# Scaling a group's samples in one step, and moving sines, residuals, sums and the last expert pick in a Trainium2 kernel

## The chip, the cores and the metric

The kernel runs on one core of one Trainium2 chip. The metric is device time in microseconds (us) of one execution. The core has a matrix engine (TensorE, PE in the profile), a vector engine (VectorE, DVE), a scalar engine for functions and copies (ScalarE, ACT), a general engine (GpSimd, POOL) and DMA queues. Each engine runs its own instructions in program order and waits on the others by semaphores. Matmuls write to PSUM, of which the kernel makes four tiles of two banks each; VectorE and ScalarE read them from there.

## The reference, cut to what matters

64 signals of 80000 samples are cut into 157 frames of 512 (L = 157, D = 512), and each frame goes through a cosine transform (DCT). One layer follows: layer normalisation, an attention by phases with a gate, and a layer of 16 experts of which each signal takes the best one.

```python
h = tokenizer(x)                              # frames @ dct.T            (64, 157, 512)
x = layernorm(h)
key_phase, query_phase = tanh(x @ Wk + bk) * pi, tanh(x @ Wq + bq) * pi
V = x @ Wv + bv
for s in range(4):                            # 4 sets of 8 planes, phasors exp(i phase)
    memory = cumsum(key_ph[s] * V, axis=1)
    total += softmax(set_weights)[s] * real(sum(memory * conj(qry_ph[s])))
retrieved_pos = ...                           # the same with phases of the position
gate = sigmoid(x @ Wg + bg)
total = gate * total + (1 - gate) * sigmoid(pos_weight) * retrieved_pos
h = h + x + (total / norm) @ Wo + bo
y = layernorm(h)
scores = softmax(mean(y, axis=1) @ Wg_ffn + bg_ffn)
idx = argmax(scores)
h = h + scores[idx] * (y @ We[idx] + be[idx])
```

## The kernel before

The signals go in 16 groups of 4 (g = 0 to 15). The tokens of a group lie in five tiles of 128 rows (n = 0 to 3 and TAIL): four signals by 32 tokens each. The DCT is folded into the weights: in group 0 the weights wv, wkq and wg are carried once into the space of the samples (`through_dct`), less their column mean, so that later products take the folded samples `xT` directly, each column times its token's `rstd`. One group's experts run beside the next groups' work, in a fixed order of instructions.

Weights lose their mean in one of two ways: by a matmul behind the transform, or by subtracting it from the raw weights:

```python
def less_mean(total, k, to):
    nc.tensor.matmul(to, tables[:, 6 + k], total, start=False, stop=True)

def centre(raw, total):
    ps = bank()
    nc.tensor.matmul(ps, mean, total, start=True, stop=True)
    sub(raw, raw, ps.unsqueeze(1).to_broadcast([P, C, D]))
```

A tile's way from the samples (the sines are copied by ScalarE, the sums are VectorE's, rstd is GpSimd's, the residual is ScalarE's), and the scaling of its samples:

```python
def embed_statistics(g, n):
    ...
    nc.scalar.copy(sines, odd[:, 1, : P + 1])
    add(by_r[:, 1, :], odd[:, 0, :P], sines[:, :P])
    sub(by_r[:, 3, :], odd[:, 0, 1 : P + 1], sines[:, 1 : P + 1])
    rstd, shift = statistics(h)          # bn_stats, bn_aggr, then rstd and shift on GpSimd
    ...
def embed_res(g, n):
    ...
    nc.scalar.activation(r, h, AF.Identity, bias=shift, scale=rstd1)

def spread(g, n, room=None):             # rstd of a tile's tokens along the free axis, on all partitions
    s["by", n] = tr = bank()[:, :P] if room is None else room
    nc.tensor.transpose(tr, s["rstd", n].to_broadcast([P, P]), ident)

def scale(g, n):
    x, tr = tile_of(s["xT"], n), s.pop(("by", n))
    nc.vector.tensor_tensor(x, x, tr.unsqueeze(1).to_broadcast([P, C, P]), ALU.mult)
```

Group 0 up to its gate (`keep` writes a tile's value and then scales that tile's samples):

```python
def first_values():
    ...
    def keep(n):
        keep_value(0, n)
        spread(0, n)
        scale(0, n)
    ...
    embed(0, 0)
    embed(0, 1)
    ps = bank()[:, : C * 2 * F].rearrange("p (c n) -> p c n", c=C)
    for k in range(C):
        through_dct(raw_kq, k, ps[:, k], stop=False)
        less_mean(total_kq, k, ps[:, k])
    embed_statistics(0, 0)
    nc.scalar.copy(wkq, ps)
    embed_statistics(0, 1)
    ...                                  # residuals, value(0, n), keep(n), embeds of the other tiles
    keep(2)
    next(consts)
    value(0, TAIL)
    fold_once(1, 0)
    centre(raw_g, total)
    keep(3)
    keep(TAIL)
    for k in range(C):
        if k % 2 == 0:
            ps = psum()
        through_dct(raw_g, k, ps[:, k % 2])
        if k % 2:
            nc.scalar.copy(wg[:, k - 1 : k + 1], ps)
    project(0)                           # keys and queries, tanh on ScalarE
    ...
    for n in range(2):
        embed(1, n)
        embed_statistics(1, n)
    phasors(0)                           # eight sines on ScalarE: four for keys, four for queries
    for n in range(2):
        embed_res(1, n)
    weigh()

def first_gate():
    made = chain(weight_sums(wo, t_o), weight_sums(wv, t_v))
    for n in range(C):
        gate_part(0, n)                  # 16 matmuls, tanh on ScalarE
        if n == 0:
            fold_twice(1, 1)
        m = n + 2
        if m < NM:
            embed(1, m)
            embed_statistics(1, m)
        if n == 1:
            scores(0)
        spread(1, n)
        scale(1, n)
        if m < NM:
            embed_res(1, m)
        add_bo(0, n)
        next(made)
        next(made)
    ...
```

The end: the last group's output sums, and the last pick, whose fetched experts end the kernel:

```python
def output_product(g, i):
    ...
    more = lambda to, x: nc.gpsimd.tensor_tensor(to, to, x, ALU.add)
    ...
    elif i == 7:
        add(second, ps, first)
        more(r22, second)
        more(r21, second)
        more(r12, first)

def expert(g, n, between=lambda c: None, spreads=()):
    ps = psum()
    for c in range(C):
        between(c)
        expert_chunk(g, n, c, ps[:, 0, :])
    ...
    expert_out(g, n, ps[:, 0, :])        # result on VectorE, then output DMAs

add_bias(g - 1, ORDER[0])                # g is the last group here
expert(g - 1, ORDER[0])
...
def routes(c):
    ...
    elif c == 3:
        route(g)
        route_sum(g)
...
def picks(c):
    if c == 1:
        route_spread(g)
        pick(g)
        fetch(g, [*flat, all_v.rearrange("p i c o -> p (i c o)")], 2, biases)

add_bias(g - 1, ORDER[1])
expert(g - 1, ORDER[1], routes)
add_bias(g - 1, ORDER[2])
expert(g - 1, ORDER[2], picks)
```

Of the kernel before, what the change touches and what calls it, by code (L numbers as in the profile page):

```python
# [51 lines left out]
def audio_tower(ctx: ExitStack, tc: tile.TileContext, a, out):  # L52
# [158 lines left out]
    def centre(raw, total):  # L211
        ps = bank()
        nc.tensor.matmul(ps, mean, total, start=True, stop=True)
        sub(raw, raw, ps.unsqueeze(1).to_broadcast([P, C, D]))
# [313 lines left out]
    def phasors(g):  # L528
        u = S[g].pop("u")
        for n, to in ((0, kf), (1, qf)):  # L530
            for k in range(2):
                rows = slice(2 * F * k + F * n, 2 * F * k + F * (n + 1))
                to_k = to.rearrange("p s b t -> p (s b t)")[:, HN * k : HN * (k + 1)]
                nc.scalar.activation(to_k[F : 2 * F], u[rows, 0], AF.Sin, scale=PI)
                nc.scalar.activation(to_k[:F], u[rows, 1], AF.Sin, bias=quarter[rows], scale=-PI)
# [75 lines left out]
    def output_product(g, i):  # L611

        s = S[g]
        ps = product(g, i, fac_o)
        (r11, r12), (r21, r22) = ([r[:, :, n : n + H] for n in (0, H)] for r in s["res2"])
        more = lambda to, x: nc.gpsimd.tensor_tensor(to, to, x, ALU.add)  # L616
        if i == 1:
            s["u"] = [p2.tile([P, 2, H], F32, tag="u", name="u") for _ in range(2)]
            nc.scalar.copy(s["u"][0], ps)
        first, second = s["u"]  # L620
        if i in (1, 2):
            add(r11, ps, r11)
        elif i == 6:
            add(first, ps, first)
        elif i == 7:
# [3 lines that stand above are left out]
            more(r12, first)  # L629
        elif i == 5:  # L630
            add(r22, ps, r22)
            if g + 1 == NG:
                add(r12, ps, r12)
            for n in (2, 3):
                statistics2(g, n)
            if g + 1 < NG:
                add(r12, ps, r12)
        elif i == 3:
            add(r12, ps, r12)
        else:  # L640
            add(r21, ps, r21)
# [154 lines left out]
    def expert(g, n, between=lambda c: None, spreads=()):  # L796

        ps = psum()
        for c in range(C):
            between(c)  # L800
            expert_chunk(g, n, c, ps[:, 0, :])
        for k, m in enumerate(spreads):
# [6 lines left out]

    def first_values():  # L810

        consts = constants()

        def keep(n):
            keep_value(0, n)
            spread(0, n)
            scale(0, n)

# [8 lines left out]
        total_kq = add_up(raw_kq, 2 * F, "sum2")  # L827
# [8 lines left out]
        ps = bank()[:, : C * 2 * F].rearrange("p (c n) -> p c n", c=C)  # L836
        for k in range(C):
            through_dct(raw_kq, k, ps[:, k], stop=False)
            less_mean(total_kq, k, ps[:, k])
        embed_statistics(0, 0)  # L840
        nc.scalar.copy(wkq, ps)
# [3 lines left out]
        value(0, 0)  # L845
        fold_once(0, 1, nc.vector)
        fold_twice(0, 1)
        value(0, 1)
        embed(0, 2)
        embed(0, 3)  # L850
        keep(0)
# [5 lines left out]
        keep(1)  # L857
        total = add_up(raw_g, D, "x2T", nc.gpsimd)
        embed(0, TAIL)
        embed_statistics(0, TAIL)  # L860
        embed_res(0, TAIL)
        value(0, 3)
        keep(2)
        next(consts)
        value(0, TAIL)
        fold_once(1, 0)
        centre(raw_g, total)
        keep(3)
        keep(TAIL)
        for k in range(C):  # L870
            if k % 2 == 0:
                ps = psum()
            through_dct(raw_g, k, ps[:, k % 2])
            if k % 2:
                nc.scalar.copy(wg[:, k - 1 : k + 1], ps)
        project(0)
        fold_twice(1, 0)
        fold_phases(0)
        next(consts)
        next(consts)  # L880
        next(consts)
        fold_once(1, 1)
        for n in range(2):
            embed(1, n)
            embed_statistics(1, n)
        phasors(0)
        for n in range(2):
            embed_res(1, n)
        weigh()

    def first_gate():

        made = chain(weight_sums(wo, t_o), weight_sums(wv, t_v))
        for n in range(C):
            gate_part(0, n)
            if n == 0:
                fold_twice(1, 1)
            m = n + 2
            if m < NM:
                embed(1, m)  # L900
                embed_statistics(1, m)
            if n == 1:
                scores(0)
            spread(1, n)
            scale(1, n)
            if m < NM:
                embed_res(1, m)
            add_bo(0, n)
            next(made)
            next(made)  # L910
        spread(1, TAIL)
        scale(1, TAIL)
        add_bo(0, TAIL)
        load_half(2, 0)
# [142 lines left out]
    add_bias(g - 1, ORDER[0])  # L1057
# [6 lines left out]

    def routes(c):
        if c == 1:
            turn_x2(g, 0)
        elif c == 2:
            turn_x2(g, 1, nc.vector.tensor_copy)
        elif c == 3:  # L1070
            route(g)
            route_sum(g)
# [10 lines left out]
    def picks(c):  # L1083
        if c == 1:
            route_spread(g)
# [6 lines left out]
    expert(g - 1, ORDER[2], picks)  # L1092
# [121 lines left out]
```

## Time and profile before

| | |
|---|---|
| time, median of 3 runs | 1423.63 us (1423.09 to 1425.6) |
| span of the profiled run | 1421.9 us |
| TensorE busy | 1405.3 us, 99% |
| VectorE busy | 997.3 us, 70% |
| GpSimd busy | 607.1 us, 43% |
| ScalarE busy | 402.0 us, 28% |
| DMA | 119.74 MB, mean 84 GB/s |

The span runs from the first to the last instruction. A line such as L288 is a line of the kernel file; matmuls are named by their output and inputs (`mm<-ident,rstd`). An entry of a timeline gives start, length, engine, line, operation, and in brackets how long the engine idled before and what released it. Group 0 fills roughly the first 110 us, a steady round of projection, values, gate, experts and attention the time to 1370, and the last group's experts the rest.

### The profile page before, as it was taken

Reading aid. Unit: us, or ns where it says so; the run is one execution under the profiler, and the core shown is the slowest. Engines: PE = TensorE matmul, PEld = TensorE weight load, DVE = VectorE, ACT = ScalarE, POOL = GpSimd, SP = SyncE. Lnnn points to the kernel's source line nnn. Section 1 sums busy time; section 2 is a strip of 40 time slices with the busy share of each in tenths; the row PEclk is TensorE's granted clock in tenths of the full one; section 3 lists DMA queues with packets and bytes.
Section 4 is the critical chain, followed back from the end, with each engine's and each line's share of the span. In section 5 each row is a group of like instructions: output and inputs, shape, how many; then the busy total and the mean of one; then the engine's idle time right before and its main releaser. Section 6 shows DMA issues by size and latency. Waiting matters only on the chain.

```text
span 1421.9 us, 26962 instructions
## 1 busy us (share of the span) xinstructions
PE 1405.3 (99%) x10646; PEld 929.2 (65%) x10646; DVE 997.3 (70%) x2090; ACT 402.0 (28%) x690; POOL 607.1 (43%) x849
## 2 busy tenths in 40 slices
PE   9899999999999999999999999999999999999998
PEld 5477576675757667575675757657586675766762
DVE  5677776777767676677777767677676777767573
ACT  2414242141422314232142422314223142421410
POOL 2354533535444255533535445255442545345322
PEclk9999999999999999999999999999999999999999
DMA  6013204032140322204132040322303232030305
GB/s 219 1 39 125 75 1 177 24 126 75 39 148 16 130 71 109 88 5 167 34 126 75 10 176 16 127 75 76 118 9 134 68 126 74 1 143 22 126 8 192
DMA packets 47485, 119.74 MB, mean 84 GB/s; under 512 B 9264, under 2 KB 26176, under 8 KB 39424
## 3 DMA queue, kind: packets, MB, share of 16 engines
q0 software_dynamic: 11072, 71.31, 13.0%
q1 hardware_dynamic: 35788, 46.06, 11.0%
q8 instruction: 85, 1.39, 0.4%
q10 hardware_dynamic: 500, 0.64, 0.2%
q14 instruction: 40, 0.33, 0.1%
HBM read 97.41 MB, written 20.58 MB: 83 GB/s over the span
## 4 chain that ended last, share of the span: by engine, by line
PE 91%; DVE 3%; POOL 3%; DMA 1%; issue 1%; ACT 0%; SPq 0%; DVEq 0%; POOLq 0%
PE mm L362 26%; PE mm L567 16%; PE mm L778 16%; PE mm L601 9%; PE mm L233 8%; PE mm L674 3%; PE mm L514 2%; PE mm L248 2%; PE mm L250 2%; PE mm L684 1%; POOL rstd L225 1%; PE mm L586 1%; PE mm L548 1%; PE mm L288 1%; DVE st L220 1%
## 5 line engine op out<-in xcount | busy, mean ns | idle before, releaser
L224 POOL TENSOR_SCALAR rstd<-mv 128x1 f32<-128x1 f32 x160 | 53.5, 334 | 536.1 <-DVE mv L222 529.7
L778 PE MATMUL mm<-we,x2T 128*32 128x512 f32 x2400 | 273.2, 595 | 0.5 <-DVE res_t L789 0.5
L778 PEld LDWEIGHTS mm<-we,x2T 128*32 128x32 f32 x2400 | 70.4, 109 | 149.1 <-issue 141.9
L97 DVE TENSOR_TENSOR gT<-mm,gT 128x128 f32<-128x128 f32 (+1 forms) x135 | 87.0, 672 | 88.5 <-PE mm L567 87.0
L609 DVE TENSOR_TENSOR gT<-mm,gT 128x320 f32<-128x320 f32 x256 | 116.9, 487 | 19.1 <-PE mm L601 14.7
L601 PE MATMUL mm<-att,v 32*128 32x192 f32 (+2 forms) x2048 | 127.8, 371 | 0.9 <-ACT res_t L277 0.5
L601 PEld LDWEIGHTS mm<-att,v 32*128 32x128 f32 x2048 | 105.5, 185 | 11.7 <-PE mm L601 2.9
L732 POOL DMA_INDIRECT we<-in_we,rows x60 | 64.3, 1072 | 105.1 <-issue 98.1
L97 DVE TENSOR_TENSOR v<-mm,v 128x512 f32<-128x512 f32 x105 | 70.9, 687 | 52.5 <-PE mm L362 52.5
L577 ACT ACTIVATE gT<-gT,hbg 128x320 f32<-128x320 f32 x120 | 59.6, 554 | 169.0 <-DVE gT L97 169.0
L225 POOL TENSOR_TENSOR rstd<-rstd,power 128x1 f32<-128x1 f32 x160 | 98.6, 616 | 13.4
L97 DVE TENSOR_TENSOR res<-mm,res 128x512 f32<-128x512 f32 x96 | 64.3, 684 | 56.5 <-POOL res L616 41.8
L277 ACT ACTIVATE res<-mm,shift,rstd 128x512 f32<-128x512 f32 x64 | 49.8, 778 | 158.7 <-POOL rstd L263 110.6
L661 ACT ACTIVATE x<-res,shift,rstd 128x512 f32<-128x512 f32 x64 | 52.1, 814 | 139.0 <-DVE res L97 121.9
L362 PE MATMUL mm<-t_o,sum 128*128 128x256 f32 x384 | 88.1, 379 | 0.0
L362 PE MATMUL mm<-t_v,sum 128*128 128x256 f32 x360 | 86.7, 384 | 0.0
L282 POOL TENSOR_TENSOR res<-res,bo 128x512 f32<-128x512 f32 x64 | 86.3, 1377 | 0.2 <-issue 0.2
L789 DVE SCALAR_TENSOR_TENSOR res<-mm,gate,res 128x512 f32<-128x512 f32 x64 | 48.0, 750 | 50.4 <-PE mm L288 36.4
L362 PEld LDWEIGHTS mm<-t_o,sum 128*128 128x128 f32 x384 | 71.9, 190 | 11.0
L616 POOL TENSOR_TENSOR res<-res,u 128x512 f32<-128x512 f32 x48 | 59.6, 1270 | 44.9 <-DVE u L97 44.9
L233 PE MATMUL mm<-wv,xT 128*128 128x512 f32 x160 | 72.0, 594 | 1.1 <-DVE xT L294 0.8
L119 POOL TENSOR_TENSOR xT<-xT 128x640 f32<-128x640 f32 x30 | 46.5, 1550 | 59.7 <-DVE even L97 40.7
(194 smaller groups left out, 2787.8 us busy)
## 6 DMA issues: line engine op xcount, KB each, us to landing
xT<-in_frames SPq DMA_DIRECT2D x32, 640.0 KB, 4.5
out<-res SPq DMA_DIRECT2D x248, 64.0 KB, 1.7
out<-res_t SPq DMA_DIRECT2D x62, 32.0 KB, 1.6
out<-res_t SPq DMA_DIRECT2D x62, 26.0 KB
wv<-in_wv SPq DMA_DIRECT2D x2, 512.0 KB, 5.7
wg<-in_wg SPq DMA_DIRECT2D x1, 1024.0 KB
wo<-in_wo SPq DMA_DIRECT2D x1, 1024.0 KB
we<-in_we,rows POOLq DMA_INDIRECT x60, 8.1
```

The costliest lines, as they stand in the source:

```text
L97: add = lambda *x: nc.vector.tensor_tensor(*x, ALU.add)
L225: nc.gpsimd.tensor_tensor(rstd, rstd, power, ALU.pow)
L233: nc.tensor.matmul(ps, tile_of(x[:, c], n), w[:, c, :], start=(c == 0), stop=(c == C - 1))
L282: nc.gpsimd.tensor_tensor(r, r, bo, ALU.add)
L362: nc.tensor.matmul(ps[:, b, :], lhs[:, c, P * b : P * (b + 1)], w[:, c, :], start=(c == 0), stop=(c == 1))
L567: nc.tensor.matmul(ps[:, o, :HN], w[:, c, o * P : (o + 1) * P], rhs[:, c], start=(c == 0), stop=(c == 1))
L577: nc.scalar.activation(to, to, AF.Tanh, bias=hbg[:, c : c + 1], scale=0.5)
L601: nc.tensor.matmul(to, s["v", n][q, c * P : (c + 1) * P], by, start=(n == 0), stop=(n == TAIL))
L609: nc.vector.tensor_tensor(th, r[:, :, n], th, op)
L616: more = lambda to, x: nc.gpsimd.tensor_tensor(to, to, x, ALU.add)
L732: nc.gpsimd.indirect_dma_start(out=ws[b][:, n * k : n * (k + 1)], out_offset=None, in_=of, in_offset=bass.IndirectOffsetOnAxis(ap=rows[:, ...
L778: nc.tensor.matmul(ps[Q * i : Q * (i + 1), :], s["x2T"][:, c, i, Q * n : Q * (n + 1)], s["ws"][i][:, c, :], start=(c == 0), stop=(c == C - 1),
```

## The change

The first group's samples are no longer scaled tile by tile. All its values are made first from unscaled samples, and `scale_all` then spreads the rstd of all five tiles by six products with the identity and scales two halves at once. The column mean of wkq is taken from the raw weights like that of wg, and both are taken earlier (`means`, `centre`). Around the first gate, the key sines come ahead of the query sines with an embedding between them, residuals move, and the sums of wv's quarters come before those of wo. In the last group, three sums go from GpSimd to VectorE and one expert bias is added earlier. The last pick follows the last chunk of an expert, ahead of that expert's result. The purpose is to keep TensorE from waiting at both ends of the kernel.

```diff
-    def centre(raw, total):
-        ps = bank()
+    def means(total, ps):
         nc.tensor.matmul(ps, mean, total, start=True, stop=True)
-        sub(raw, raw, ps.unsqueeze(1).to_broadcast([P, C, D]))
+    def centre(raw, ps, n):
+        sub(raw, raw, ps.unsqueeze(1).to_broadcast([P, C, n]))
@@ output_product
-        more = lambda to, x: nc.gpsimd.tensor_tensor(to, to, x, ALU.add)
+        last = g + 1 == NG
+        more = lambda to, x: (nc.vector if last else nc.gpsimd).tensor_tensor(to, to, x, ALU.add)
         if i in (1, 2):
             add(r11, ps, r11)
+            if last and i == 2:
+                add_bias(g - 1, ORDER[0])
@@ expert
             expert_chunk(g, n, c, ps[:, 0, :])
+        between(C)
@@ new
+    def scale_all(g):
+        s = S[g]
+        ps = psum()
+        for m in range(2):
+            lo = 0
+            for n, w, at in ((0, P, 0), (1, P, 0), (TAIL, HT, 0)) if m == 0 else ((TAIL, HT, HT), (2, P, 0), (3, P, 0)):
+                nc.tensor.matmul(ps[:, m, lo : lo + w], s["rstd", n].to_broadcast([P, P]),
+                                 ident[:, at : at + w], start=True, stop=True)
+                lo += w
+        for m in range(2):
+            x = half(s["xT"], m)
+            nc.vector.tensor_tensor(x, x, ps[:, m, :HN].unsqueeze(1).to_broadcast([P, C, HN]), ALU.mult)
@@ first_values, from the embeds of tiles 0 and 1 on (the new order; cut)
+        embed_statistics(0, 0)
+        embed_statistics(0, 1)
+        embed_res(0, 0)
+        embed_res(0, 1)
+        value(0, 0)
+        ps = psum()
+        mean_kq, new_kq = ps[:, 0, : 2 * F], ps[:, 1, : C * 2 * F].rearrange("p (c n) -> p c n", c=C)
+        means(add_up(raw_kq, 2 * F, "sum2"), mean_kq)
+        centre(raw_kq, mean_kq, 2 * F)
+        fold_once(0, 1, nc.vector)
+        fold_twice(0, 1)
+        total = add_up(raw_g, D, "x2T", nc.gpsimd)
+        value(0, 1)
+        for k in range(C):
+            through_dct(raw_kq, k, new_kq[:, k])
+        nc.scalar.copy(wkq, new_kq)
+        ...                              # keep_value(0, n) in place of keep(n); embeds, values 2
+        mean_g = bank()
+        means(total, mean_g)
+        centre(raw_g, mean_g, D)
+        value(0, 3)
+        value(0, TAIL)
+        keep_value(0, 3)
+        next(consts)
+        keep_value(0, TAIL)
+        scale_all(0)
+        made = [psum(), psum()]
+        for k in range(C):
+            through_dct(raw_g, k, made[k // 2][:, k % 2])
+        nc.scalar.copy(wg[:, :2], made[0])
+        fold_once(1, 0)
+        fold_twice(1, 0)
+        fold_once(1, 1)
+        project(0)
+        nc.scalar.copy(wg[:, 2:], made[1])
+        fold_phases(0)
+        phasors(0, (0,))
+        next(consts)
+        next(consts)
+        embed(1, 0)
+        embed_statistics(1, 0)
+        phasors(0, (1,))
+        embed_res(1, 0)
+        next(consts)
@@ first_gate
+        made = chain(weight_sums(wv, t_v), weight_sums(wo, t_o))
+        gate_part(0, 0)
+        embed(1, 1)
+        embed_statistics(1, 1)
+        embed_res(1, 1)
+        weigh()
+        fold_twice(1, 1)
+        deviations(0)                    # spread(1, 0), scale(1, 0)
+        add_bo(0, 0)
+        weights()                        # two steps of the weight sums
+        gate_part(0, 1)
+        scores(0)
+        embed(1, 2)
+        embed_statistics(1, 2)
+        deviations(1)
+        embed_res(1, 2)
+        add_bo(0, 1)
+        weights()
+        gate_part(0, 2)
+        for n in (3, TAIL):
+            embed(1, n)
+            embed_statistics(1, n)
+        for n in (3, TAIL):
+            embed_res(1, n)
+        deviations(2)
+        add_bo(0, 2)
+        weights()
+        gate_part(0, 3)
+        add_bo(0, 3)
+        deviations(3)
+        deviations(TAIL)
+        add_bo(0, TAIL)
+        weights()
@@ the end
-    add_bias(g - 1, ORDER[0])
     expert(g - 1, ORDER[0])
     def routes(c):
         ...
         elif c == 3:
             route(g)
             route_sum(g)
-    def picks(c):
-        if c == 1:
+        elif c == C:
             route_spread(g)
             pick(g)
             fetch(g, [*flat, all_v.rearrange("p i c o -> p (i c o)")], 2, biases)
     expert(g - 1, ORDER[1], routes)
     add_bias(g - 1, ORDER[2])
-    expert(g - 1, ORDER[2], picks)
+    expert(g - 1, ORDER[2])
```

## The prediction, as it stood before the run

> **What bounds the kernel now.** I read the page's first part, then the waits of TensorE, then the timelines of the first 96 us and of the last 40. The page:
>
> ```profile
> PE 1405.3 (99%) x10646; PEld 929.2 (65%) x10646; DVE 997.3 (70%) x2090; ACT 402.0 (28%) x690; POOL 607.1 (43%) x849
> ```
>
> TensorE (PE) is busy for 1405.3 of 1421.9 us. From 130 to 1330 us it idles 1.3 us, and the change does not touch that stretch. All that can be won lies in the first 90 us and the last 50. TensorE's waits in the first 96 us ("waited for: total, times, longest"):
>
> ```profile
> PE mm L248 <- issue: 2.6, 1, 2.6
> PE mm L288 <- DVE wg L96: 2.4, 1, 2.4
> PE mm L185 <- POOL ident masks.py:199: 1.4, 1, 1.4
> ...
> PE mm L233 <- DVE xT L294: 0.8, 1, 0.8
> PE mm L601 <- ACT res_t L277: 0.5, 1, 0.5
> ```
>
> L288 is the spreading of a tile's rstd over the partitions: tile 3's stood 2.36 us (43.2 to 45.6) because VectorE (DVE) was centring the gate's weights (L96, 2.29 us), and its bank came free behind that. The largest gap, 61.2 to 63.85, stands before group 1's third tile, behind the sines and residuals on ScalarE (ACT). It costs more than itself, as busy times and granted clock (column after POOL) in stretches of 2 us show:
>
> ```profile
> 62.00:64.00 2.00, 0.15 (x1) 0.18 (x2) 1.20 (x3) 1.53 (x3) 1.81 (x3) 1.00 0.00 0
> 64.00:66.00 2.00, 1.90 (x9) 1.46 (x10) 1.16 (x3) 1.25 (x2) 0.69 (x2) 0.81 0.00 0
> 66.00:68.00 2.00, 2.00 (x6) 1.39 (x5) 0.20 (x1) 1.76 (x3) 0.00 (x0) 0.50 0.00 0
> ```
>
> The gate part that follows takes 5.57 us in the chain instead of 4.31. Before the first read of the values (84.34) I add up, from the waits and the chain: 0.15 + 0.78 + 0.27 + 2.36 + 0.28 + 2.63 + 0.52 waiting, 0.26 (L250 at 16.38, 0.71 instead of 0.45), about 0.5 (L250 at 64.75, on the folding) and 1.26 of slow clock: 9.0 us.
>
> At the end the chain runs through the pick, the fetch and the last expert's matmuls:
>
> ```profile
> 1392.44 7.80 DMA t_v<-in_we,rows
> 1400.24 0.04 issue
> 1400.28 17.37 PE mm L778 x154
> ```
>
> TensorE has finished group 6 at 1395.6 and stands 0.27, 0.90 and 0.44 us for three of the four fetched experts. From 1400.28 it is dense, so the end lies 17.4 + 4.2 us behind the landing of the fourth. VectorE's timeline ahead of the fetch:
>
> ```profile
> 1384.08 0.32 DVE L691 TENSOR_REDUCE tot<-mm 128x1 f32<-128x157 f32 x1 [1.48 <-PE mm L684]
> 1384.94 0.75 DVE L789 SCALAR_TENSOR_TENSOR res<-mm,gate,res 128x512 f32<-128x512 f32 x1 [0.54 <-PE mm L778]
> 1385.61 0.74 DVE L772 SCALAR_TENSOR_TENSOR res<-be,gate,res 128x512 f32<-128x512 f32 x1
> 1386.27 0.22 DVE L708 SCALAR_TENSOR_TENSOR logit<-mm,rbg 128x64 f32<-128x64 f32 x1
> ```
>
> The sums are there at 1384.4, but the pick (L708 on) stands behind an expert's result and the next bias.
>
> **What the Trainium skill says.** "TensorE: Matmul & The Clock Gate", Part 1, has the array fall to half its clock after an idle window of about 3.4 us; here a gap of 2.63 us with sparse work behind it gave 0.50 already, so new gaps of 2 us or more are suspect. "ScalarE: Activation LUTs", What ACT_TABLE_LOAD costs, gives about 1.28 us a load; every load in the trace takes 1.28. Its section on table sets puts cheap functions into every set, and the trace shows no load before a copy or Identity, so sines split by a copy need one load as before. "DMA: Bandwidth & Descriptors", Issuing engines are not separate DMA queues, has all queues share 16 engines; the trace shows them 0.92 to 1.04 busy from 1392 to 1400, so outputs moved into that time delay the fetch.
>
> **The change part by part.**
>
> **Work.** Five spreadings (L288, 0.12 us each in the chain) leave the first values; six identity products, four of 128 columns and two of 64, each two passes of 0.11 or 0.06, come in: 4 x 0.22 + 2 x 0.12 = 1.1, so +0.5 us of TensorE. The eight less-mean matmuls of wkq (0.11 each) leave for two: -0.7. That nets to -0.2. VectorE exchanges five scalings of 0.68 for two of 1280 elements; 1024 take 1.23 and 2048 take 2.29, so some 1.5 each: 3.0 for 3.4. Hardly any work goes; the change must live from waits.
>
> **First values.** I replayed the new order with the trace's durations. The wkq block (17.98 to 20.16 before) moves behind the first values, so value 0 starts near 17.75; VectorE's second statistics start at 18.8 instead of 20.77, because ScalarE's sines no longer stand behind the wkq copy. TensorE then runs value 1 to 25.0, wkq to 26.3, embeds to 28.1, value 2 to 31.6, TAIL's embed to 32.5, the gate's means to 33.3, value 3 to 36.8. VectorE centres wg from 35.8 to 38.1, now beside values instead of before a spreading. Value TAIL may wait 0.7 us for TAIL's residual (ACT, 37.4) and ends at 40.9; the six products end at 42.0, wg's transform (5.43) at 47.4 against 51.6 before, the projection (2.2) at 49.6. The second wg copy, now behind tanh, ends at 51.2. Share (1.0) and one embed (0.9) fill the time, and the first gate part starts at 51.5. Before, it started at 56.74 with one more embed (0.9) behind it: **4.3 us ahead** here.
>
> **First gate.** Here I expect no gain. ScalarE runs the key sines from 52.5, the sines' copy of tile 0, the query sines to 56.9, tile 0's residual (behind POOL's rstd) to 58.8, a table load to 60.1 and tanh to 60.9. TensorE, through its first part at 55.85 and an embed at 56.75, needs tile 0's bank for the next part and stands until 58.8: about 2 us. Tile 1's sines wait for tanh, so VectorE idles until 61.2 and then has no break: statistics, weigh, folding, scaling, two weight sums, two for the scores, and so on, with small waits of TensorE at 66, 73 and 79 (0.6 to 1.3 each, on banks freed by residuals). I get the first read at 80.65 instead of 84.34 (-3.7) and VectorE's first product with the gate (L609) at 82.9 instead of 87.47 (-4.6). L609 sets the reads' pace, 16 x 0.485, so the second counts more: **-4.2 us**.
>
> **Last group's sums.** POOL's three sums take 3.72 us (1368.71 to 1372.43), and VectorE waits 2.61 for the second. On VectorE they take 3 x 0.69 = 2.1, and the next sum starts at 1370.7 instead of 1371.23: -0.5. The bias (L772, 0.72) moves into idle time. So TensorE's 0.45 us wait on res_t (1378.2) goes: **-0.5**.
>
> **Last pick.** The spread of the sums follows chunk 3 directly (0.9 earlier) and the pick follows it on VectorE instead of 0.75 + 0.74 of other work. It starts near 1384.8 instead of 1386.27: with the 0.5 above, 1.5 earlier, and POOL's first fetch too. Against that, this expert's result comes out some 3.3 us behind the pick, at 1388.8, and its 256 KB leave inside the fetch's time instead of before it. At the 270 to 290 GB/s shown there this is up to 0.9 us. I take half: **-1.0 us** at the end, the 0.5 included (TensorE still waits for the data).
>
> Sum: 1423.6 - 4.2 - 1.0 = **1418.4 us**.
>
> **Rivals.** (1) **The gate's new order gives the front's gain back**: TensorE's new stop near 57 lets the clock fall (1.3 us lost, as before), or the chain ScalarE-VectorE-POOL is longer than replayed. For it: ScalarE's table load before tanh stands between two statistics, and small POOL operations have taken double beside VectorE's folding (L224 0.69 at 22.44, else 0.21). Against it: after that stop TensorE has slack, since VectorE is behind. It leaves 1 to 2 us of the front: about 1421. (2) **The fetch is bound by bytes**: starting it earlier then wins nothing. For it: the busy share near 1. Against it: from 1388 to 1390 it was 0.10, room that an earlier start uses. It makes 1419.4. (3) **All gaps close**: the 9.0 us go and the end gives 1.5, so 1413. Against it: the bank that TensorE needs at 57 hangs on a residual which I cannot place before 58. (4) **A bank held too long**: experts' results now leave later, and a fifth tile could stop TensorE; but only one of four is held, so I give it little.
>
> **Range and chances.** The front may give 2 to 6, the end 0 to 1.8. Long replays err towards too much gain, so the range reaches further up: 1415.3 to 1421.5. The three runs before spread over 2.5 us. Faster by over 2% would need 28 us, more than the 16.6 us that TensorE idles in all: 0.01. Slower by over 2% would need a new standstill of 28 us: 0.01. Within 2%: 0.98.
>
> **What would show it.** TensorE's busy time stays within 1 us of 1405; its waits on "DVE wg" (2.4) and on issue before L248 (2.6) are gone; wg's transform ends near 47.4; a wait of 1.5 to 2 us on a residual stands before the second gate part; the first read comes at 80 to 81. At the end, the pick starts near 1380.6 (1386.27 - 4.2 - 1.5), before the expert's result, with no POOL sums in the last group; from the pick to the fourth expert's landing it is now 14.0 us, and I expect 14.5. A gap over 2.6 us with the clock at 0.5 in the gate, or a first read later than 82.5, would prove the front wrong; a landing 15.5 us or more behind the pick would prove the end wrong.

## The result and the profile after

| | before | after |
|---|---|---|
| time, median of 4 runs each | 1424.33 us (1423.09 to 1425.6) | 1418.99 us (1418.3 to 1421.01) |
| ratio after / before, 95% interval | | 0.9965 (0.9948 to 0.9982) |
| span of the profiled run | 1421.9 us | 1419.2 us |

The change makes the kernel 0.35% faster, about 5 us. The profiled run of after is the longest of its four; why will turn out below. First the engines on its page:

```profile
PE 1404.2 (99%) x10647; PEld 929.9 (66%) x10647; DVE 1002.4 (71%) x2091; ACT 401.5 (28%) x690; POOL 602.9 (42%) x846
```

TensorE's busy time fell by 1.1 us only; VectorE's rose by 5.1 and GpSimd's fell by 4.2. Hardly any work went, and the rest of the 2.7 us between the spans are waits. TensorE's waits of after in the first 96 us (total, times, longest):

```profile
PE mm L250 <- ACT res L279: 1.5, 1, 1.5
PE mm L185 <- POOL ident masks.py:199: 1.4, 1, 1.4
PE mm L605 <- ACT res_t L279: 1.1, 1, 1.1
PE mm L552 <- ACT res L279: 1.0, 1, 1.0
PE mm L250 <- DVE xT L97: 1.0, 1, 1.0
PE mm L290 <- POOL rstd L227: 0.5, 2, 0.4
```

The two large ones of before, on the centring of wg (2.4) and the one put down to issue (2.6), are gone. None is over 1.5. New is a wait of 1.0 on a folding (`DVE xT`), and before the first read (L605) 1.1 stands instead of 0.5. What that stop does is seen in after's busy times by stretches (PE, PEld, DVE, ACT, POOL, then the granted clock of TensorE, DMA share, GB/s):

```profile
80.00:82.00 2.00, 0.83 (x5) 0.43 (x5) 2.00 (x4) 1.34 (x2) 1.90 (x5) 1.00 0.29 44
82.00:84.00 2.00, 2.00 (x26) 1.75 (x26) 2.00 (x2) 0.12 (x1) 2.00 (x2) 0.66 1.00 357
84.00:86.00 2.00, 2.00 (x28) 2.00 (x26) 0.65 (x3) 0.00 (x0) 2.00 (x2) 0.50 0.69 255
86.00:88.00 2.00, 2.00 (x48) 1.96 (x46) 1.62 (x4) 0.00 (x0) 2.00 (x3) 0.98 0.00 0
```

The clock no longer falls at 64, where the page of before had 0.81 and 0.50, but at 82 to 86. There the reads run at about half their pace: 26 and 28 matmuls in 2 us instead of 48. At the end, the chain of waits of after:

```profile
1389.71 7.82 DMA t_v<-in_we,rows
1397.52 0.04 issue
1397.57 17.37 PE mm L785 x154
```

It has the same form as before, 2.7 us earlier. The milestones of both traces, in us from the start of the span, split the gain:

| milestone | before | after | change |
|---|---|---|---|
| first embedding matmul | 15.77 | 15.98 | +0.21 |
| projection of group 0 starts | 51.53 | 48.76 | -2.77 |
| first gate part starts | 56.74 | 53.07 | -3.67 |
| first read of the values | 84.34 | 81.49 | -2.85 |
| VectorE's first product with the gate | 87.47 | 85.39 | -2.08 |
| first output product of group 0 ("product") | 93.64 | 91.74 | -1.90 |
| pick (`logit` on VectorE) | 1386.27 | 1383.53 | -2.74 |
| fourth fetched expert's first matmul | 1400.28 | 1397.57 | -2.71 |
| end | 1421.9 | 1419.2 | -2.7 |

So in this execution the front gives 1.9 us (2.1 counted from the first embedding, which starts 0.21 later) and the stretch from the product to the pick 0.84 (1292.63 to 1291.79). The gate's half of the front gives back 1.8 us of the 3.67 won by then; 0.9 of that is an embed that was only moved behind the first gate part.

### The profile page after: what moved, and what is told of

The parts are those of the page before. It is cut to its first block, busy times and chain, and to the rows that moved or that the text cites. A ratio compares the mean times of both kernels' runs of the same rounds, so it can differ in the third digit from the quotient of the medians.

```text
span 1419.2 us, 26967 instructions
## 1 busy us (share of the span) xinstructions
PE 1404.2 (99%) x10647; PEld 929.9 (66%) x10647; DVE 1002.4 (71%) x2091; ACT 401.5 (28%) x690; POOL 602.9 (42%) x846
## 4 chain that ended last, share of the span: by engine, by line
PE 90%; DVE 3%; POOL 3%; issue 1%; DMA 1%; ACT 1%; SPq 0%; DVEq 0%; POOLq 0%
PE mm L364 27%; PE mm L571 16%; PE mm L785 16%; PE mm L605 9%; PE mm L235 8%; PE mm L681 3%; PE mm L516 3%; PE mm L250 2%; PE mm L252 2%; POOL rstd L227 1%; PE mm L691 1%; PE mm L590 1%; DVE st L222 1%; PE mm L290 1%; POOL rstd L226 1%
## 5 line engine op out<-in xcount | busy, mean ns | idle before, releaser
L97 DVE TENSOR_TENSOR gT<-mm,gT 128x128 f32<-128x128 f32 (+1 forms) x135 | 87.0, 672 | 88.5 <-PE mm L571 87.0
L613 DVE TENSOR_TENSOR gT<-mm,gT 128x320 f32<-128x320 f32 x256 | 116.8, 487 | 20.7 <-PE mm L605 16.2
L605 PE MATMUL mm<-att,v 32*128 32x192 f32 (+2 forms) x2048 | 129.1, 374 | 1.1 <-ACT res_t L279 1.1
L605 PEld LDWEIGHTS mm<-att,v 32*128 32x128 f32 x2048 | 107.1, 187 | 11.7 <-PE mm L605 3.0
L97 DVE TENSOR_TENSOR v<-mm,v 128x512 f32<-128x512 f32 x105 | 70.9, 688 | 52.9 <-PE mm L364 52.9
L97 DVE TENSOR_TENSOR res<-mm,res 128x512 f32<-128x512 f32 x96 | 64.4, 684 | 54.1 <-POOL res L621 39.2
L621 POOL TENSOR_TENSOR res<-res,u 128x512 f32<-128x512 f32 x45 | 55.9, 1269 | 42.1 <-DVE u L97 42.1
L364 PEld LDWEIGHTS mm<-t_v,sum 128*128 128x128 f32 x360 | 64.8, 190 | 10.7 <-issue 3.5
```

What stands on the lines that cost most here:

```text
L97: add = lambda *x: nc.vector.tensor_tensor(*x, ALU.add)
L364: nc.tensor.matmul(ps[:, b, :], lhs[:, c, P * b : P * (b + 1)], w[:, c, :], start=(c == 0), stop=(c == 1))
L605: nc.tensor.matmul(to, s["v", n][q, c * P : (c + 1) * P], by, start=(n == 0), stop=(n == TAIL))
L613: nc.vector.tensor_tensor(th, r[:, :, n], th, op)
```

## The experiments

Runs of one block shared a chip and the runs of before made there. Below, "front" is the time from the first embedding matmul to the product; it is 77.87 us before and 75.76 after. From the product to the pick it is 1292.63 and 1291.79.

### Which part brings it: e1 to e4

**e1_front_only** keeps the new values and the new gate, with the old end. Edit against the changed kernel, cut:

```diff
-        more = lambda to, x: (nc.vector if last else nc.gpsimd).tensor_tensor(to, to, x, ALU.add)
+        more = lambda to, x: nc.gpsimd.tensor_tensor(to, to, x, ALU.add)
-            if last and i == 2:
-                add_bias(g - 1, ORDER[0])
-        between(C)
-        elif c == C:                     # the pick, in routes of ORDER[1]
+    def picks(c):                        # back in ORDER[2]
+        if c == 1:
```

> The change's front (values and gate of group 0), with the end of the kernel before: sums on GpSimd, bias and pick at their old places. Theory (the front brings most of the gain, and a fall of TensorE's clock ahead of the first read takes part of it back in some executions): group 0's first output product starts at 89.5 to 92 instead of 93.6 us, from there to the end 1328 us as before, 1419.0 to 1420.5 in all. Rival (the end brings most): 1422.5 or more.

Measured: 1420.18 us against 1424.98, ratio 0.9969 (0.9959 to 0.998). Front 73.85, product to pick 1292.57. The front holds 4.0 us in this profile, twice what after's own shows with the same code there, and the times agree with it: 4.4 us.

**e2_tail_only** is the kernel before with the new `output_product`, `expert` and end: the pluses and minuses of e1 exchanged, with the old `first_values` and `first_gate`.

> The kernel before with only the end of the change: three sums on VectorE, bias earlier, pick ahead of the expert's result. Theory: the first output product at 93.6 as before; from there to the end 0.8 us less than before, because the pick comes 0.9 earlier; 1423.4 for a before of 1424.3. Rival (the end brings most): 4 us less than before. Rival (the fetch is bound by bytes): no change.

Measured: 1424.62 against 1424.98, ratio 1.0 (0.9992 to 1.0009). Product to pick 1291.80, as in after, and the pick to the fourth expert 14.21. The 0.83 us are there in the trace; in the times an effect of 0.0006 cannot be told from none. This profile shows a second fall of the clock, in the old values:

```profile
46.00:48.00 2.00, 2.00 (x4) 0.83 (x3) 2.00 (x5) 0.00 (x0) 0.00 (x0) 0.65 0.00 0
48.00:50.00 2.00, 2.00 (x4) 0.71 (x3) 1.23 (x3) 0.00 (x0) 0.00 (x0) 0.50 0.00 0
```

It follows the 2.4 us wait on the centring of wg. The profile of before has that wait without the fall.

**e3_values_only** keeps the new values up to `scale_all`; the projection's stage, the gate and the end are old.

```diff
         scale_all(0)
-        made = [psum(), psum()]
-        ...                              # new order
-        phasors(0, (0,))
-        embed(1, 0)
-        embed_statistics(1, 0)
-        phasors(0, (1,))
+        ...                              # old order of transform, folds, project
+        for n in range(2):
+            embed(1, n)
+            embed_statistics(1, n)
+        phasors(0)
```

> The change's values (all values first, scaling in one step, means of both weights early), then the projection, sines and first gate in the old order, old end. Theory (the values close the 2.4 us wait on the centring and the small ones, the gate's order closes its gap of 2.6 us with the slow clock behind it): the projection starts 2.9 us earlier (48.8), the gap ahead of group 1's third tile stays at 2 to 3 us with the clock at 0.5 behind it; 2.5 to 3.5 us less than before. Rival (the new gate brings nothing): as the whole front, e1.

Measured: 1421.15 against 1424.98, ratio 0.9971 (0.996 to 0.9981). From the first embedding to the projection it takes 34.12 us (before 35.76, after 32.78). Up to there the code differs from after's only in what stands behind `scale_all`; what differs ahead of that is the clock, which falls here behind the 0.99 us wait on the folded half. Busy times of e3:

```profile
26.00:28.00 2.00, 1.02 (x6) 0.82 (x6) 1.97 (x4) 0.37 (x1) 0.38 (x1) 1.00 0.91 338
28.00:30.00 2.00, 1.90 (x10) 1.77 (x9) 1.97 (x5) 0.27 (x1) 0.00 (x0) 0.57 0.12 24
30.00:32.00 2.00, 2.00 (x7) 1.23 (x7) 1.74 (x6) 0.27 (x1) 0.78 (x2) 0.58 0.00 0
```

The gap of 2.63 before group 1's third tile is still there too, with the slow clock behind it (0.60 and 0.55 from 62 to 66): front 75.49.

**e4_gate_only** is the counterpart: old values, then from `made = [psum(), psum()]` on the new order and the new gate; old end.

> The values of the kernel before (scaled tile by tile, wkq with less_mean), then the change's projection, sines and first gate, old end. Theory: the projection starts as before (51.5 to 52), the gap of 2.6 us is split into several of 0.4 to 1.5 us, and 0 to 2 us are won, depending on the clock. Rival (the gate brings all): 4 us less than before. Rival (the new gate loses): 1 us more than before.

Measured: 1424.26 against 1424.98, ratio 0.9995 (0.9987 to 1.0004). From the projection to the product 41.08 us, as in e1 (41.09); before 42.11, e3 41.37. The big wait stays where it was, and here too the clock falls behind it, so that wg's transform takes 7.11 us instead of 5.42. TensorE's timeline of e4, with the spreading that waits and the transform behind it:

```profile
45.69 0.29 PE L290 MATMUL mm<-ident,rstd 128*128 128x128 f32 x1 [2.36 <-DVE wg L96]
46.26 7.11 PE L196 MATMUL mm<-wg,tables 128*128 128x512 f32 x12 [0.28 <-DVE v L413]
```

What follows from the four: **the values bring most of it** (0.29% of 0.35% by the times). They remove the wait on wg and with it the fall of the clock that follows it in some executions. How much falls of the clock weigh is seen in e4, which keeps the wait. Its thirteen executions form groups by their mean granted clock, of which one fall (about 1.7 us of 1420) takes 0.0012: four at 1.0 take 1422.33 to 1422.41 us, six at 0.999 take 1423.88 to 1425.29, three at 0.998 take 1425.26 to 1427.01. The gate's order by itself is too small for the times; in the traces it brings up to 1.0 us from the projection to the product. On top of the values the medians of e3 and e1 give it another 1.0 us, which is within their scatter.

### What is left in front: e5, e6, e8

The new wait of 1.0 in the values has a cause that VectorE's and GpSimd's timelines of after show side by side. VectorE:

```profile
21.91 0.82 DVE L97 TENSOR_TENSOR even<-xT 128x640 f32<-128x640 f32 x1
22.76 2.85 DVE L119 TENSOR_TENSOR xT<-xT 128x640 f32<-128x640 f32 x1
25.64 1.44 DVE L97 TENSOR_TENSOR xT<-even 128x320 f32<-128x320 f32 x1
```

GpSimd:

```profile
21.96 2.97 POOL L203 TENSOR_TENSOR total<-wg 128x1024 f32<-128x1024 f32 x1
25.01 1.73 POOL L204 TENSOR_TENSOR total<-total 128x512 f32<-128x512 f32 x1
```

The foldings took 0.83 and 0.49 before. Beside GpSimd's two additions for the sum over wg, which also read two operands each, they take 2.85 and 1.44. Hardly any of their work is done beside them: the first folding ends 0.68 us behind GpSimd's first addition, the second 0.34 behind its second. TensorE has run ahead by then and stands for the folded half:

```profile
27.34 0.69 PE L250 MATMUL mm<-dct_e,xT 128*128 128x128 f32 x4 [0.98 <-DVE xT L97]
```

This is what the Trainium skill has under "SBUF — State Buffer", Who interferes with whom: a VectorE instruction with two inputs in SBUF contends with a GpSimd instruction that reads SBUF.

**e5_sum_on_vector** moves the sum of wg to VectorE, later:

```diff
         fold_twice(0, 1)
-        total = add_up(raw_g, D, "x2T", nc.gpsimd)
         value(0, 1)
         ...
         embed_statistics(0, 3)
+        total = add_up(raw_g, D, "x2T")
```

> The changed kernel with the row sums of wg on VectorE, behind tile 3's statistics where VectorE idled 2.5 us, instead of on GpSimd beside VectorE's folding. Theory (the first folding step took 2.85 and the next 1.44 us instead of 0.82 and 0.49 because GpSimd's sum, 2.97, ran beside it): the folding is back at 0.82 and 0.49, TensorE's wait of 1.0 us at 27.3 goes, and the projection starts 1 us earlier, 1 us less in all (1418). Rival (the wait at 27.3 has another cause, or the sum now delays the means): the projection no earlier than 48.5.

Measured: 1420.57 against 1425.3, ratio 0.9971 (0.9961 to 0.9982). The collision is gone; VectorE's timeline of e5:

```profile
22.11 0.82 DVE L119 TENSOR_TENSOR xT<-xT 128x640 f32<-128x640 f32 x1
22.97 0.49 DVE L97 TENSOR_TENSOR xT<-even 128x320 f32<-128x320 f32 x1
```

So is TensorE's wait, and the third tile's value starts 1.8 us earlier (12.05 us behind the first embedding instead of 13.83). Two new waits follow, on the sum that VectorE now makes and on a residual (TensorE's timeline of e5):

```profile
32.08 1.10 PE L213 MATMUL mm<-total,mean 128*128 128x512 f32 x2 [0.21 <-DVE total L204]
33.77 7.13 PE L235 MATMUL mm<-wv,xT 128*128 128x512 f32 x16 [0.59 <-ACT res L279]
```

So the projection starts 32.0 us behind the first embedding instead of 32.78. Yet the front ends no earlier: 73.94, against 73.91 in e7, whose front is the changed kernel's. The 0.8 us are lost before the read, where GpSimd computes the last tile's rstd beside VectorE's sums of wo (GpSimd's timeline of e5):

```profile
77.48 0.72 POOL L226 TENSOR_SCALAR rstd<-mv 128x1 f32<-128x1 f32 x1 [0.43 <-issue]
78.28 1.00 POOL L227 TENSOR_TENSOR rstd<-rstd,power 128x1 f32<-128x1 f32 x1
```

The same two take 0.21 and 0.57 for the tile before. TensorE waits 0.89 for this rstd and then 1.03 for the residual behind it. The cause of the wait on the folding is shown, and removing it wins nothing by itself: a wait on the last tile's rstd takes its place. That the sums of wo slow this rstd is argued from the overlap; 0.43 us of its delay stand ahead of it, with nothing in the profile that it waited for.

**e6_sines_together** takes the split of the sines back:

```diff
-        phasors(0, (0,))
+        phasors(0)
         ...
-        phasors(0, (1,))
```

> The changed kernel with the eight sines of keys and queries in one row again, ahead of the copy of tile 0's sines. Theory (the split lets tile 0's statistics run 2 us earlier): the copy at 58 instead of 55.9, TensorE's stop ahead of the second gate part grows from 1.0 to about 3 us, the clock falls behind it, and the first output product comes 1 to 3 us later. Rival (the split is worth nothing, because VectorE and ScalarE are behind anyway): within 0.5 us at the first output product.

Measured: 1422.93 against 1425.3, ratio 0.9985 (0.9976 to 0.9993). ScalarE copies the next tile's sines behind all eight functions, at 57.69 instead of 55.92, and the rstd and the residual follow as much later. ScalarE's timelines of after and of e6:

```profile
55.92 0.24 ACT L260 COPY sines<-mm 128x129 f32<-128x129 f32 x1
```

```profile
57.69 0.24 ACT L260 COPY sines<-mm 128x129 f32<-128x129 f32 x1
```

TensorE's timeline of e6:

```profile
60.55 0.32 PE L290 MATMUL mm<-ident,rstd 128*128 128x128 f32 x1 [2.46 <-POOL rstd L227]
61.91 6.14 PE L552 MATMUL mm<-xT,wg 128*128 128x320 f32 x16 [1.04 <-ACT res L279]
```

The stop of 0.35 + 1.04 in after becomes 2.46 + 1.04. The clock falls to 0.50 behind it, and the gate part takes 6.14 us instead of 4.57. Front 76.03: 2.1 us worse than e7 beside it. The order of the sines carries the gate's new order: without it the change keeps less than half its gain.

**e8_kept_busy** fills the stop before the read with five identity products into the free second bank of the PSUM tile that takes the last tile's rstd:

```diff
-        def deviations(n):
-            spread(1, n)
+        def deviations(n, busy=0):
+            ps = psum()
+            spread(1, n, ps[:, 0, :P])
+            for _ in range(busy):
+                nc.tensor.matmul(ps[:, 1, :P], ident, ident, start=True, stop=True)
-        deviations(TAIL)
+        deviations(TAIL, 5)
```

> The changed kernel with five small matmuls more, into a free bank, in TensorE's stop of 1.1 to 1.3 us ahead of the first read. Theory (the clock falls there in some executions, to 0.58 from 82 to 86 in the profiled one, and costs 2 us): the clock stays at 1.0 from 80 to 88 and no execution is 2 us slower than the fastest; the first output product at 89 to 90; the median 0.5 to 1.5 us below the changed kernel's. Rival (the clock falls for what came before, or costs nothing since VectorE sets the reads' pace): median and spread as in the changed kernel.

Measured: 1421.32 against 1425.3, ratio 0.9974 (0.9965 to 0.9983). The stop shrinks to 0.18 and the clock stays at 1.00; as it also stays there in three profiles without the filling (below), this does not show that the filling held it. But the scaling of the last tile waits for the extra products, and the sum of wo behind it slides into GpSimd's additions of bo (VectorE's timeline of e8):

```profile
80.92 0.69 DVE L296 TENSOR_TENSOR xT<-xT,mm 128x512 f32<-128x512 f32 x1 [0.21 <-PE mm L925]
81.52 1.68 DVE L96 TENSOR_TENSOR t_o<-wo,t_o 128x512 f32<-128x512 f32 x1
83.12 1.75 DVE L96 TENSOR_TENSOR t_o<-wo 128x512 f32<-128x512 f32 x1
84.80 3.25 DVE L613 TENSOR_TENSOR gT<-mm,gT 128x320 f32<-128x320 f32 x7
```

In after the first of these two sums takes 0.98; the second takes 1.75 in every profile with the new gate, and no run moved it. The first product with the gate (L613) comes 69.07 us behind the first embedding, 1.1 later than in e7 (67.99), and the front ends 1.1 later too (74.97 against 73.91). The median was expected below the changed kernel's; it is 2.1 us above e7's, of which 0.63 is e7's bias. A clock that holds helps only if VectorE is not made later for it.

### The end: e7 and e12

**e7_bias_later** adds the early bias one product later (the products run in the order 1, 2, 6, 7):

```diff
-            if last and i == 2:
-                add_bias(g - 1, ORDER[0])
         elif i == 6:
             add(first, ps, first)
+            if last:
+                add_bias(g - 1, ORDER[0])
```

> The changed kernel with the early expert bias of the last group one product later (behind product 6 instead of product 2). Theory (behind product 2 it delays the token sum that TensorE waits for 0.4 us, which gives back what it won): that wait goes, and from the first output product to the pick 0.5 us less than in the changed kernel. Rival (the bias is in idle time either way): no difference, and a wait of the same size moves elsewhere.

Measured: 1419.26 (1419.1 to 1421.11) against 1425.3, ratio 0.996 (0.9947 to 0.9974). Product to pick 1291.16, 0.63 less than after. In after, VectorE's timeline has the bias (L779) ahead of a sum that TensorE needs:

```profile
1362.60 0.69 DVE L97 TENSOR_TENSOR res<-mm,res 128x512 f32<-128x512 f32 x1
1363.21 0.74 DVE L779 SCALAR_TENSOR_TENSOR res_t<-be,gate,res_t 128x512 f32<-128x512 f32 x1
1363.87 0.68 DVE L96 TENSOR_TENSOR sum<-gT 128x512 f32<-128x512 f32 x1
```

TensorE's timeline of after:

```profile
1364.70 1.97 PE L364 MATMUL mm<-t_o,sum 128*128 128x256 f32 x8 [0.41 <-DVE sum L96]
```

In e7 VectorE takes that sum (`sum<-gT`) directly behind the L97, and TensorE has no wait there at all. VectorE's timeline of e7:

```profile
1360.42 0.69 DVE L97 TENSOR_TENSOR res<-mm,res 128x512 f32<-128x512 f32 x1
1361.03 0.68 DVE L96 TENSOR_TENSOR sum<-gT 128x512 f32<-128x512 f32 x1
```

**e12_pick_back** takes the pick back to where it was:

```diff
-        elif c == C:
+    def picks(c):
+        if c == 1:
             route_spread(g)
             pick(g)
             fetch(...)
-    expert(g - 1, ORDER[2])
+    expert(g - 1, ORDER[2], picks)
```

> The changed kernel with the last pick back at its old place, behind the expert's result and one chunk of the next expert; the sums on VectorE and the earlier bias stay. Theory (the end's gain is the pick's alone, because the bias gave back what the sums won): from the first output product to the pick 1292.6 us as in the kernel before, 0.8 more than in the change. Rival (the sums won): 1292.1 or less.

Measured: 1419.52 against 1424.25, ratio 0.9966 (0.9952 to 0.9979). Product to pick 1292.66: what it was before the change. VectorE's timeline of e12 has the old order, a result and a bias ahead of the pick:

```profile
1379.80 0.32 DVE L698 TENSOR_REDUCE tot<-mm 128x1 f32<-128x157 f32 x1 [1.48 <-PE mm L691]
1380.66 0.75 DVE L796 SCALAR_TENSOR_TENSOR res<-mm,gate,res 128x512 f32<-128x512 f32 x1 [0.54 <-PE mm L785]
1381.33 0.74 DVE L779 SCALAR_TENSOR_TENSOR res<-be,gate,res 128x512 f32<-128x512 f32 x1
1381.98 0.22 DVE L715 SCALAR_TENSOR_TENSOR logit<-mm,rbg 128x64 f32<-128x64 f32 x1
```

In after the pick stands 1.25 us behind the sums, held only by its own matmul:

```profile
1382.28 0.32 DVE L698 TENSOR_REDUCE tot<-mm 128x1 f32<-128x157 f32 x1 [1.48 <-PE mm L691]
1383.53 0.23 DVE L715 SCALAR_TENSOR_TENSOR logit<-mm,rbg 128x64 f32<-128x64 f32 x1 [0.94 <-PE mm L704]
...
1386.78 0.73 DVE L796 SCALAR_TENSOR_TENSOR res<-mm,gate,res 128x512 f32<-128x512 f32 x1
```

So the pick is the whole 0.84 us of the end, and the rest nets to zero: the early bias takes 0.63 (e7), so the sums on VectorE bring as much. No run has those sums without a moved bias. The times of e2 and e12 are too coarse for 0.8 us; this rests on the traces, which agree to 0.1 us (1292.57 to 1292.66 in the five with the old pick, 1291.71 to 1291.81 in the seven with the new pick and the early bias).

### The clock before the first read, and the parts put together: e9 to e11

**e9_change_again** is the changed kernel, unchanged.

> The changed kernel unaltered, beside the three below. Theory (the 2 us of slow clock ahead of the first read come in some executions only): in an execution without it the first output product starts 73.9 us behind the first embed, as in e1, e5 and e7, against 75.8 in the first profile of the change. If the 15.3 us from pick to fourth expert (14.0 in the first profiles) are the chip's and not the edits', they are here too when they are in the other three. Rival (the edits lengthened it): 14.0 here.

Measured: 1420.02 (1418.56 to 1420.6) against 1424.25, ratio 0.9965 (0.9951 to 0.9979). The clock falls again, 0.53 and 0.62 from 82 to 86, and the front is 75.74. Five of the profiled runs have the same instructions up to the read:

| run | wait before the read | clock 82 to 84, 84 to 86 | front |
|---|---|---|---|
| after | 1.10 | 0.66, 0.50 | 75.76 |
| e9 | 1.10 | 0.53, 0.62 | 75.74 |
| e1 | 1.28 | 1.00, 1.00 | 73.85 |
| e7 | 1.30 | 1.00, 1.00 | 73.91 |
| e12 | 1.10 | 1.00, 1.00 | 74.05 |

The same stop lets the clock fall in two and not in three, and **the fall costs 1.8 us** (75.75 less 73.94). That is why the profile of after, the longest of its four runs, shows 2.7 us where the times show 5. The profile of before adds to it: its mean clock is 0.998, while 34 of the 67 executions of before beside the experiments have 0.997 or less and are 1.6 to 1.8 us longer than those at 0.998 (24), by the medians of each block (the nine at 0.999 lie between). The nine of the changed kernel (after and e9) have 0.998 or 0.999. So part of the 5 us is, by these means, fewer falls of the clock. It is no count of them, as a fall behind the last matmul, which costs nothing, is in the mean too.

**e10_sums_earlier** clears VectorE's way to the last tile by taking a step of the sums of wo ahead of its statistics:

```diff
         add_bo(0, 1)
         weights()
+        weights()
         gate_part(0, 2)
         ...
         add_bo(0, 2)
-        weights()
```

> The changed kernel with the third pair of weight sums one place earlier, where VectorE idled 1.9 us, instead of beside TAIL's rstd on GpSimd. Theory (those sums, two inputs from SBUF, slow GpSimd's rstd of TAIL, whose residual holds the bank that the first read waits for; and they stand ahead of the first product with the gate): the stop ahead of the read shrinks from 1.1 to 1.3 to under 0.6 us and the first output product comes 0.7 to 1.5 us earlier (72.4 to 73.2 behind the first embed). Rival (VectorE's sum of work sets it, wherever the sums stand): 73.7 to 74.1.

Measured: 1420.25 against 1424.25, ratio 0.9971 (0.9959 to 0.9984); front 73.89, no better than e1. TensorE's timeline of e10 at the read:

```profile
79.67 0.38 PE L290 MATMUL mm<-ident,rstd 128*128 128x128 f32 x2
80.91 2.09 PE L605 MATMUL mm<-att,v 32*128 32x320 f32 x26 [0.85 <-ACT res_t L279]
```

The stop is 0.85 still: VectorE now idles 0.96 before the scaling, which waits for TensorE's spreading, and TensorE waits for the residual. The rival's number came out, but not its reason, since VectorE has idle time there.

**e11_all_three** is e5, e7 and e10 together.

> The changed kernel with wg's row sums on VectorE (e5), the third pair of weight sums earlier (e10) and the bias one product later (e7). Theory: the parts add up, 0.8 + 1 + 0.6, so 71.6 to 72.6 us from the first embed to the first output product and 1291.2 from there to the pick; 2 to 2.5 us below the changed kernel, 1416.5 to 1417.5. Rival (they share one wait and only the largest counts): 1 us below.

Measured: 1418.01 (1417.76 to 1418.83) against 1424.25, ratio **0.9952** (0.9939 to 0.9966). It is the fastest kernel of the study, 2.0 us below the changed kernel beside it (1420.02), though their intervals against before overlap. Front 73.46 (71.6 to 72.6 was expected), product to pick 1291.06. The bias adds its 0.65; the two edits in front add 0.4 to 0.6 where each alone added 0.2 at most, and no fall of the clock shows in its profile (of the stops that let it fall elsewhere, the one on the folding is gone, the one before the read is 1.04). The mean clock of its five executions is 0.999 (two) or 1.0 (three), that of e9's is 0.998 (two) or 0.999 (three), so fewer falls are probably part of the 2.0 us; how these divide stays open.

## Why the prediction was right, step by step

Its total, 1418.4, lies 0.6 us below the measured 1418.99, and most of its mechanisms show. That it came so close is in part luck. Several terms were off and made up for each other. And the sum was drawn from one execution of before in which the clock fell once, where half of the others lose 1.6 to 1.8 us more, and it has no fall in after, where two of the profiled executions lose 1.8 (after and e9).

- **Work**: right. TensorE's busy time is within 1.1 us of before.
- **First values**: right in mechanism, too large in size. The waits on wg and on issue are gone, and one more embedding lies behind the gate's start. But it was put at "4.3 us ahead"; measured is 2.8 (56.74 to 53.07, less 0.9 for the embed). The term that failed is the duration of the foldings of the second half, replayed from a trace in which only small GpSimd operations ran beside them. GpSimd's sum over wg, named in the change and not costed, made them 3.0 us longer. The third tile's value started at 29.81 instead of 28.1 for it (0.98 of waiting, and an embed whose second half took 1.08 instead of 0.61), and without it 1.8 earlier (e5); wg's transform ended at 48.8, not near 47.4. In e3's profile the clock fell behind that stop as well and took 1.3 more. `scale_all` itself took 1.44 us a half where 1.5 was predicted.
- **First gate**: "no gain" was nearly right and hid two opposite things. With the clock held, projection to product is 1.0 us shorter (e4, e1); with the fall in after it is 0.9 longer (42.98). The stop before the second gate part is 0.35 + 1.04 us, a little under the predicted 1.5 to 2. From the first embedding to the first read it is 65.3 to 65.5 us in the five same fronts, where the prediction's 80.65 makes 64.9 (less the 15.77 of before).
- **The front's sum**: -4.2 predicted; the traces give -4.0 without the fall (e1) and -2.1 with it.
- **Last group's sums**: -0.5 predicted, -0.63 by way of e7. The wait on res_t is gone. "The bias moves into idle time" failed: it delays a sum for the next product and costs 0.63.
- **Last pick**: the collision that was to cost 0.5 of the 1.5 did not come. Pick to fourth expert took 14.04 us (before 14.01). This expert's result did follow 3.3 us behind the pick as predicted, and its output left inside the fetch's time. In sum -0.84 for -1.0: the early bias took what the collision did not.

Of the rivals, the first (the gate gives the gain back) was half right: the clock does fall and takes 1.8 us, but in some executions only, and before the read, not near 57. There TensorE stood 1.0 us in every one of the five same fronts and the clock held. e6 shows what a longer stop there costs: with 2.46 + 1.04 us the clock falls, and the front is 2.1 us longer. The second (bytes bind the fetch) falls: the landing moved with the pick, 14.04 us behind it in after, 13.94 in e12 with the old pick. The third falls because the gaps follow each other: what e5 took away came back 50 us later. The fourth left no trace: TensorE had no wait on a bank in the last group.

## What to carry to other kernels

When an order is replayed with durations from a trace, look for each VectorE operation with two inputs at what GpSimd reads beside it in the new order; a small sum moved there can treble an operation on the path. After removing a wait, follow the milestones to the end of the stage: e5, e8 and e10 each shortened a wait and won nothing by the end of the front. Where two executions of the same instructions differ by 2 us, compare the granted clock by stretches before looking for a cause in the code.

## What the runs showed of the hardware

- The granted clock can fall behind short stops, and behind the same stop it does so in one execution and not in another: 1.1 us before the read in two of five (above), 1.0 us on the folding in one of nine (e3), the 2.4 us on wg in two of three (e2 and e4, not before), the 2.6 us gap in three of three (before, e2, e3), 2.46 + 1.04 us in e6. Behind stops of 1.0 at 60 and 1.5 at 67 in the new gate order it never fell. The Trainium skill ("TensorE: Matmul & The Clock Gate", Part 1) names an idle window of about 3.4 us; these runs show falls behind much less. The falls cost about the same clock, whatever the stop: by the columns above, 2 x (0.34 + 0.50 + 0.02) = 1.72 us in after, 2 x (0.43 + 0.42) = 1.70 in e3, 2 x (0.35 + 0.50) = 1.70 in e2, which is some 3.4 us at half the clock.
- VectorE and GpSimd slow each other: the folding of 640 elements went from 0.83 to 2.85 us, that of 320 from 0.49 to 1.44, a sum of 512 from 0.68 to 1.75, and GpSimd's rstd power from 0.57 to 1.13 on 128x1 elements.
- In e5 to e8, which shared a chip, pick to fourth expert took 15.24 to 15.27 us (in the ten other profiles 13.6 to 14.2), and waits stand there that the profile puts down to no instruction of the kernel. The waits of e7 from 1380 to 1408, all engines:

```profile
DVE res L796 <- remote: 7.9, 2, 6.2
...
PE mm L785 <- issue: 2.5, 3, 1.1
```

The DMA engines are 0.94 to 1.04 busy in e7 from 1388 to 1400, and 0.90 to 1.04 in e9, which shows no such waits and 13.94 us. What stalled the engines was not tried and stays open. In e7's profile, the longest of its five executions, the clock also falls from 1396 to 1400 (0.52 and 0.63).
